# An adaLN block with a state-space mixer and eight experts: identity matmuls at the start, the first norm planned first, one more early slot, late loads in a new order

## The chip, the cores and the metric

The kernel runs on one core of one Trainium2 chip. The metric is the device time of one execution in microseconds. The core has five engines, each with its own instruction queue that it works off in order: PE (matmuls), DVE (vector), ACT (scalar and activation), POOL (GpSimd) and SP (which here only starts DMAs). In the trace PEld is PE's loading of the stationary operand.

## The reference

All data are float32. `x` holds B = 8 sequences of L = 512 tokens with D = 256 features; `c` holds one conditioning vector for each sequence.

```python
mod = (silu(c) @ wmod).reshape(8, 6, 1, 256)
sa, ca, ga, sb, cb, gb = (mod[:, i] for i in range(6))
ga, gb = (sign(g) * max(|g|, 0.25) for g in (ga, gb))     # with sign(0) = 1

h  = layernorm(x) * (1 + ca) + sa
x  = x + ga * attn(h)
h  = layernorm(x) * (1 + cb) + sb
x  = x + gb * ffn(h)

def attn(x):                                 # a state-space mixer, 512 inner features
    xn = layernorm(x) * gamma + beta
    u, z = split(xn @ W_in.T)                # 512 and 512
    xc = silu(depthwise_causal_conv(u, 4 taps) + conv_b)
    # state (16 numbers): s_t = s_{t-1} @ A.T + u_t @ Bm.T
    y  = (xc + s @ Cm) * sigmoid(z)
    return x + y @ W_out.T

def ffn(x):                                  # 4096 tokens, 8 experts, 1024 hidden features
    top_p, top_i = top_k(softmax(x @ wr + br), 2)
    gate = top_p[:, 0] / (top_p[:, 0] + top_p[:, 1])
    e = top_i[:, 0]                          # each token goes to one expert
    return gate * (gelu(x @ w1[e] + b1[e]) @ w2[e] + b2[e])
```

## The kernel before

**The plan.** Nearly the whole program is written against a `Plan` (line 30 on), an object that looks like the core and only records instructions with their tiles. `order()` (line 191) then makes a list schedule: it has a modelled length for each instruction, follows tile dependences, PSUM and SBUF buffers and a modelled DMA wire, and takes at each step, over all engines, the instruction that can start earliest, and among equal starts the one with the earliest due time. Due times are set in the code by `nc.due = ...` and handed back along dependences. Instructions are emitted sorted by their planned start; the chip does not see due times, only the order in each engine's queue. `plan.wanting(done=[...])` adds tiles that an instruction is to come behind in the plan. There are two plans: one for everything up to the router, one for the experts.

**First plan: mixer and router, batch by batch.** At the start `load_x`, the modulation weights `wm0`, `wm1` and the projection weights `wi`, `wo` are loaded. `three()` (line 482) makes the modulation vectors: for batch 0 on all 128 partitions at once (`s0`, tiles `pm`, `pg`, result `bc0`), and in `vectors()` (line 513) for all batches, into the scratch tensors `mod_d` and `modb_d`, from which later batches load their `bc`. `vectors()` makes the router's vectors too (`pf`, `modT`, `rw`, `rsum`, `wr2`). `states()` (line 590) prepares the state space: powers of A by repeated squaring (`at`, each step a PE product `pa` and a copy), tables `lt`, `lx`, `cs`, `wb`, `lm`, and `bw`, the product of `W_in` with `Bm`. It has 35 small copies on DVE. Then, for each batch, `stage_norm` (line 735) makes two layer norms (`xn`, `h`, then `xnT`, features on partitions; the power -1/2 runs on POOL), `stage_base` a base term, `stage_conv` projects `u` (tile `px`), convolves on DVE (`sv`) and scans the state, `stage_out` projects `z`, combines and multiplies with `W_out` (tile `po`), norms again (`xr`) and picks the expert (`oh`), and `stage_place` counts places and scatters the token numbers into `ids_d` with indirect DMAs from POOL, four for each batch, and stores the rows in `xp_d`. The code orders `states()`, `vectors()`, then the batches, with due times PERIOD = 36 us apart.

**Slots.** The expert part works in slots: a pair slot is 256 tokens of one expert, a single slot 128. For a slot, `name_tokens` (line 1023) loads its token numbers `ids` from `ids_d` on SP's queue, `rows_of` gathers the rows `xg` on POOL's, `expert_of` (line 1035) loads `w1t`, `b1t`, `b2t`, `w2t` (two megabytes) on SP's, `features` makes `hg` and transposes it to `hT` (tile `tp`), `layer1` multiplies into `ph` and takes gelu into `gl`, `layer2` multiplies into `py`, makes `ot` and scatters it to the output.

After FEW = 6 of 8 batches `early_table()` (line 958) already fixes the first NEARLY = 3 pair slots from the tokens seen so far. Slot 0's first layer is part of the first plan, and so are the gathers of slots 0 and 1. After batch 8 a late table is computed on DVE (tiles `cum`, `unit`, `done`, `mine`, `ef`, `ei`), and the other slots follow it: 13 pair slots and 4 singles always, three more singles under a condition. Weights have four buffers (`wts`), besides those of slot 0.

**Second plan.** `fetched(i)` (line 1150) is `expert_of` plus `rows_of`. `got` lists the slots fetched ahead; `work()` (line 1289) goes through the slots with `ahead = len(got)` slots in flight, names the tokens of one more, and writes for each slot `features` of the next, `layer1`, and `layer2` of the one before.

In the trace most instructions carry L154 or L159, the two lines of `Plan.add` that issue a recorded instruction (L154 where several calls are joined), so the tile names tell the groups apart. SP's dynamic loads carry their own lines: L1028 token numbers, L1041 `w1t`, L1048 `w2t`. A float32 matmul shows as two PE instructions.

Of the kernel before, what the change touches and what calls it, by code (L numbers as in the profile page):

```python
# [10 lines left out]
FP = mybir.dt.float32  # L11
# [7 lines left out]
P = 128  # L19
# [16 lines left out]
class Plan:  # L36
# [20 lines left out]
    def __init__(self, tc, last=None):  # L57

        self.tc, self.nc = tc, tc.nc
        self.free = {q: last.free[q] if last else 0.0 for q in self.REACH}  # L60
        self.ops, self.touched, self.tiles = [], {}, {}
        self.due, self.also, self.pairing = 0.0, ([], []), 0
        for name in self.QUEUES:
            setattr(self, name, self.Engine(self, name))

# [125 lines left out]
    def order(self):  # L191
        ops = self.ops
# [6 lines left out]
        start = [0.0] * len(ops)  # L199
# [11 lines left out]
        order, table = [], 2  # L211

        def may(o):

# [8 lines left out]
                at = max(at, sorted(slots[tag])[len(names) - 1])  # L223
            return at

        while len(order) < len(ops):
            best = None
            for q, l in ready.items():
                for o in l:
                    at = may(o)  # L230
                    if at is None:
                        continue
                    at = max(at, free[q])
                    if o.get("table") not in (None, table):
                        at += 1.3
                    if best is None or (at, o["due"]) < best[:2]:
                        best = (at, o["due"], o)
            assert best is not None, "no buffer for any instruction that could be next"
            at, _, o = best
# [8 lines left out]
            free[o["queue"]] = at + o["length"]  # L248
            end = at + o["length"]
            if o["size"]:  # L250
                if o["indirect"]:
                    end += 9.0
                else:
                    wire = max(wire, end) + o["size"] / 300e3
                    end = wire
            done[o["i"]] = end
            o["at"] = at
            order.append(o)
            for n in o["uses"]:
                if o["i"] in self.tiles[n][1]:  # L260
                    self.tiles[n][1].discard(o["i"])
                    left[n] -= 1
                    o_end = end + self.reach(o)
                    t = self.tiles[n][0]
                    self.ends = getattr(self, "ends", {})
                    self.ends[n] = max(self.ends.get(n, 0.0), o_end)
                    if left[n] == 0:
                        slots[t.tag].append(self.ends[n])
            for j in o["after"]:
                a = ops[j]  # L270
                start[j] = max(start[j], end + (0.05 if a["queue"] == o["queue"] and not o["size"] else self.reach(o)))
                missing[j] -= 1
                if missing[j] == 0:
                    ready[a["queue"]].append(a)
# [15 lines left out]
def adaln_mamba_moe_kernel(  # L290
# [28 lines left out]
    JB = BLK // P  # L319


    FEW, NEARLY = 6, 3
    assert (FEW * NT - E) // 2 + 1 >= NEARLY


# [105 lines left out]
    with tc.tile_pool(name="wa", bufs=1) as wa, tc.tile_pool(  # L431
# [158 lines left out]
        def states():  # L590


            for j in range(STEPS - 1):
                pa = ps_s.tile([DS, 2, DS], FP, name="pa", tag="ps")
                for s in range(2):
                    nc.tensor.matmul(
                        pa[:, s], lhsT=at[:, j, 1 - s], rhs=at[:, j, s], start=True, stop=True
                    )
                nc.vector.tensor_copy(at[:, j + 1], pa)
            i16 = ident[0:DS, 0:DS]  # L600
            a3t = wa.tile([DS, DS], FP, name="a3t")
            pa3 = ps_s.tile([DS, DS], FP, name="pa3", tag="ps")
            nc.tensor.matmul(pa3, lhsT=at[:, 0, 1], rhs=at[:, 1, 0], start=True, stop=True)
            nc.vector.tensor_copy(a3t, pa3)
            power = [i16, at[:, 0, 0], at[:, 1, 0], a3t, at[:, 2, 0]]


# [2 lines left out]
            nc.vector.memset(lt, 0.0)  # L610
            for i in range(CH):
                for j in range(i + 1):
                    nc.vector.tensor_copy(lt[:, i, j * SP : j * SP + DS], power[i - j])
                nc.vector.tensor_copy(lt[:, i, DS : 2 * DS], power[i + 1])
# [8 lines left out]
            for i, (l, r) in enumerate((  # L623
# [4 lines left out]
            nc.vector.tensor_copy(more[:, 0:5], pmo)  # L628
            pm28 = ps_s.tile([DS, DS], FP, name="pm28", tag="ps")
            nc.tensor.matmul(pm28, lhsT=at[:, 4, 0], rhs=more[:, 0], start=True, stop=True)  # L630
            nc.vector.tensor_copy(more[:, 5], pm28)
# [8 lines left out]
            nc.vector.tensor_copy(wb[:, :, DS:], pw1)  # L640

            gaps = [at[:, 5, 0], at[:, 6, 0], more[:, 3], at[:, 7, 0], at[:, 8, 0], more[:, 4]]
            lx = wa.tile([DS, len(gaps), 2 * DS], FP, name="lx")
            nc.vector.memset(lx, 0.0)
            for j, m in enumerate(gaps):
                nc.vector.tensor_copy(lx[:, j, DS:], m)
            ix = wa.tile([DS, 2 * DS], FP, name="ix")
            nc.vector.memset(ix, 0.0)
            nc.vector.tensor_copy(ix[:, DS:], i16)
            pm2 = ps_s.tile([2 * DS, len(gaps), 2 * DS], FP, name="pm2", tag="ps")  # L650
# [3 lines left out]
            nc.vector.tensor_copy(lm, pm2)  # L654

            wx = wxo[:, 1].rearrange("p (j d) -> p j d", j=KI)
            for g in range(KI // 2):
# [10 lines left out]
            pb = ps_s.tile([P, KD, DS], FP, name="pb", tag="ps")  # L668
# [6 lines left out]
            nc.vector.tensor_copy(bw[:, :, 0:DS], pb)  # L675

            return cs, wb, lm, bw

# [337 lines left out]
        def loads(fn, outs, ins, length):  # L1016

            if nc is plan:
                plan.call("sync", fn, outs, ins, length)
            else:  # L1020
                fn()

        def name_tokens(i):
            jb, at_ = tiles(i), where[i][1]

            def fn():
                o = chip.sync.value_load(at_, min_val=0, max_val=E * TOK)
                chip.sync.dma_start(  # L1028
                    out=ids[:, i, 0:jb],
                    in_=ids_d[bass.ds(o, jb * P), :].rearrange("(p j) o -> p (j o)", j=jb),  # L1030
                )
# [106 lines left out]
    with tc.tile_pool(name="g", bufs=2) as gp, tc.tile_pool(  # L1138
# [8 lines left out]
        nc.due = behind + 4 * SLOT  # L1147
        turn = count_from()

        def fetched(i, xg=None):  # L1150
            t = expert_of(
                i, wts.tile([P, KD, FF], FP, name="w1t"), wts.tile([P, KF, D], FP, name="w2t"),
                blk.tile([P, KF], FP, name="b1t"), blk.tile([P, D], FP, name="b2t"),
            )
# [12 lines left out]

        half = tab.tile([1, 2 * E], I32, name="half")
# [120 lines left out]
        def work(slots, got, begun=None):  # L1289
# [96 lines left out]
```

## Time and profile before

| | |
|---|---|
| median of 3 runs | 596.09 us (595.05 to 597.38) |
| the profiled execution | 595.11 us |
| its span in the profile | 593.2 us, so 1.9 us lie outside the span |
| PE busy | 564.6 us (95%), 2882 instructions |
| DVE, ACT, POOL busy | 351.0, 210.7, 209.4 us |
| mean granted clock of PE | 0.974 of full speed |
| DMA | 96.73 MB, 163 GB/s on average |

A line of the timeline reads: start, duration (both us), engine, line of the kernel, operation, output tile <- input tiles, shape, how many alike were merged, and in brackets how long the engine had idled before and what ended the idling. SPq is SP's DMA-issuing queue. In the page's slices one digit stands for 1/40 of the span (14.8 us), in tenths of busy time or, in the row of the clock, in tenths of full speed. Where PE is busy nearly always, the time is set by what PE has to do, by its idle stretches and by the clock that it is granted.

### The profile page before, as it was taken

The page shows a single profiled execution, that of the slowest core. Times are in us where ns is not written, and L with a number is a line of the kernel's source. Part 1 is how long each engine was busy: PE and PEld are TensorE (multiplying, and loading weights), DVE is VectorE, ACT ScalarE, POOL GpSimd, SP SyncE. Part 2 cuts the span into 40 slices and gives each one's busy share as a digit, 9 for nine tenths or more (in the row PEclk, how much of TensorE's full clock was granted, in tenths as well). Part 3 has the DMA queues.
Part 4 walks back from the last instruction along what each step waited for, and adds up shares of the span by engine and source line. Part 5 has one row for each costly group of instructions (what it writes and reads, how often), then busy time and mean ns, then how long its engine had stood idle before and what let it go on. Part 6 is the DMA issues. An engine that isn't in the chain of part 4 may idle for free. (4 is left out here: it accounts for less than half of the span.)

```text
span 593.2 us, 8692 instructions
## 1 busy us (share of the span) xinstructions
PE 564.6 (95%) x2882; PEld 430.7 (73%) x2882; DVE 351.0 (59%) x1087; ACT 210.7 (36%) x404; POOL 209.4 (35%) x334
## 2 busy tenths in 40 slices
PE   5999999999999999999999875999999999999996
PEld 2454766767575776767478764888988988988895
DVE  4879978988887678585876524434341533533212
ACT  2328544445463634341522220221322222232140
POOL 1422663636345461631334132432332222331111
PEclk9779999999999999999999896999999999999998
DMA  7347999310300101010645999699977887794000
GB/s 275 125 146 181 279 258 242 74 60 1 98 1 1 38 2 36 1 37 1 203 128 167 165 288 341 190 374 380 317 253 236 295 282 243 253 326 163 24 18 20
DMA packets 58703, 96.73 MB, mean 163 GB/s; under 512 B 9852, under 2 KB 41854, under 8 KB 58656
## 3 DMA queue, kind: packets, MB, share of 16 engines
q1 hardware_dynamic: 50720, 72.98, 41.2%
q0 software_dynamic: 7936, 23.17, 11.5%
q8 instruction: 24, 0.39, 0.4%
q14 instruction: 23, 0.19, 0.2%
HBM read 86.42 MB, written 22.81 MB: 184 GB/s over the span
## 5 line engine op out<-in xcount | busy, mean ns | idle before, releaser
L159 ACT ACTIVATE gl<-ph,b1t 128x256 f32<-128x256 f32 (+1 forms) x152 | 68.5, 452 | 187.9 <-PE ph L154 186.0
L154 PE MATMUL py<-w2t,gl 128*128 128x256 f32 x476 | 110.2, 384 | 0.0
L154 PEld LDWEIGHTS py<-w2t,gl 128*128 128x128 f32 x476 | 92.1, 193 | 13.1
L159 POOL DMA_INDIRECT out<-ot,ids x36 | 37.1, 1030 | 158.1 <-DVE ot L159 140.7
L159 DVE SCALAR_TENSOR_TENSOR sv<-u,pt,sv 128x512 f32<-128x512 f32 x96 | 77.1, 809 | 13.0 <-ACT sv L159 12.7
L159 PE MATMUL ph<-hT,w1t 128*128 128x256 f32 (+1 forms) x304 | 84.2, 359 | 0.0
L154 PE MATMUL ph<-hT,w1t 128*128 128x256 f32 (+1 forms) x304 | 84.2, 359 | 0.0
L159 DVE TENSOR_TENSOR ot<-py,b2t 128x256 f32<-128x256 f32 x34 | 14.4, 424 | 113.1 <-PE py L154 110.1
L159 PE MATMUL px<-xnT,wi 128*128 128x512 f32 x128 | 69.6, 626 | 0.0
L154 PE MATMUL px<-xnT,wi 128*128 128x512 f32 x128 | 66.0, 597 | 0.0
L159 POOL DMA_INDIRECT xg<-xp_d,ids x36 | 38.6, 1073 | 62.7 <-DMA ids<-ids_d 42.3
L154 PEld LDWEIGHTS ph<-hT,w1t 128*128 128x128 f32 x304 | 55.6, 191 | 6.3
L159 PEld LDWEIGHTS ph<-hT,w1t 128*128 128x128 f32 x304 | 55.1, 191 | 5.9
L159 POOL DMA_INDIRECT ids_d<-tok,row x32 | 34.7, 1084 | 36.1 <-DVE row L159 13.7
L154 PEld LDWEIGHTS px<-xnT,wi 128*128 128x128 f32 x128 | 24.6, 192 | 31.2 <-issue 31.2
L159 ACT COPY u<-px 128x512 f32<-128x512 f32 x32 | 18.7, 585 | 63.4 <-PE px L154 63.4
L159 ACT ACTIVATE tz<-px 128x512 f32<-128x512 f32 x32 | 19.1, 596 | 40.3 <-PE px L154 36.7
L159 PEld LDWEIGHTS px<-xnT,wi 128*128 128x128 f32 x128 | 21.3, 192 | 16.4 <-issue 14.6
L159 POOL TENSOR_TENSOR rs<-ve,nhalf 128x4 f32<-128x4 f32 x16 | 19.4, 1217 | 38.7 <-DVE ve L159 28.8
L159 DVE COPY hT<-tp 128x512 f32<-128x512 f32 (+1 forms) x20 | 12.7, 634 | 34.2 <-PE tp L154 33.9
L159 DVE TENSOR_TENSOR hg<-hg,xg 128x256 f32<-128x256 f32 x72 | 28.8, 422 | 1.2
L159 DVE TENSOR_TENSOR xr<-po,h 128x256 f32<-128x256 f32 x32 | 13.5, 421 | 25.6 <-PE po L154 25.3
(347 smaller groups left out, 947.4 us busy)
## 6 DMA issues: line engine op xcount, KB each, us to landing
w1t<-in_w SPq DMA_DIRECT2D x19, 1024.0 KB, 8.2
w2t<-in_w SPq DMA_DIRECT2D x19, 1024.0 KB, 5.6
xp_d<-modb_d SPq DMA_DIRECT2D x8, 1536.0 KB, 21.2
xp_d<-xr SPq DMA_DIRECT2D x8, 520.0 KB, 4.6
xt<-in_x SPq DMA_DIRECT2D x8, 512.0 KB, 11.6
bc<-mod_d SPq DMA_DIRECT2D x7, 384.0 KB, 3.5
b2t<-in_b SPq DMA_DIRECT2D x19, 128.0 KB, 8.3
w<-in_w SPq DMA_DIRECT2D x2, 1024.0 KB
```

The source lines that it names most:

```text
L154: me["calls"].append(lambda: getattr(getattr(self.nc, name), op)(*args, **kw))
L159: calls=[lambda: getattr(getattr(self.nc, name), op)(*args, **kw)],
```

## The change

1. `Plan.order()` gets two more settings. `hold = 24`: as long as an engine's earliest possible start lies before 24 us (planned time), it takes, among what can start within 0.3 us of that, the instruction with the earliest due time. `warm = (20.0, 7.8, 0.47, filler)`: before 20 us of planned time, each planned gap of PE is filled to 80% with matmuls of the identity with itself (256 columns, tile `pwarm`, read by nobody); a matmul is planned at 0.47 us, and before 7.8 us, where lengths are doubled, at 0.94.
2. `stage_norm(0)` is written first, with due time 20. `states()` follows, and `vectors()` and `stage_base(0)` come behind `xnT` of batch 0.
3. In `states()` the 35 copies move from DVE to ACT, and `pw1`, `pm2`, `pb` move from a PSUM pool of one buffer to that of `px` with three.
4. `NEARLY` goes from 3 to 4, so 12 pair slots are left to the late table.
5. Slot 1 is fetched first; then the numbers of the first late slot (now slot 4) are named, and slots 2 and 3 are fetched behind these in the plan. In `work()` each later slot's numbers are named behind the `w1t` of the slot fetched last.

```diff
@@ Plan.order()
-        while len(order) < len(ops):
+        while len(order) < len(ops) + fillers:
...
-                    if best is None or (at, o["due"]) < best[:2]:
-                        best = (at, o["due"], o)
+                    could.append((at, o["due"], o["i"], o))
+                if could:
+                    mine = min(could)
+                    if mine[0] < self.hold:
+                        mine = min((c for c in could if c[0] < mine[0] + 0.3), key=lambda c: c[1:3])
+                    if best is None or mine[:3] < best[:3]:
+                        best = mine
...
+            length = o["length"]
+            if self.warm and o["queue"] == "PE" and at < self.warm[0]:
+                slow = 2 if at < self.warm[1] else 1
+                n = int(0.8 * (at - free["PE"]) / (slow * self.warm[2]))
+                if n > 0:
+                    order.append(dict(i=-1, at=free["PE"], queue="PE", calls=[self.warm[3]] * n))
+                    fillers += 1
+                length *= slow
@@
-    FEW, NEARLY = 6, 3
+    FEW, NEARLY = 6, 4
@@ vectors()
             for half, to in ((0, mod_d), (1, modb_d)):
+                nc.due = (1 + 2 * half) * PERIOD
...
+            nc.due = 3 * PERIOD
@@ states(), 35 copies in all
-                nc.vector.tensor_copy(at[:, j + 1], pa)
+                nc.scalar.copy(at[:, j + 1], pa)
...
-            pw1 = ps_s.tile([P, SPAN[0], DS], FP, name="pw1", tag="ps")
+            pw1 = ps_x.tile([P, SPAN[0], DS], FP, name="pw1", tag="px")
@@
-        def name_tokens(i):
+        def name_tokens(i, behind=()):
...
-            loads(fn, [ids[:, i, 0:jb]], [at_, *id_views[: FEW * NT]], 0.8)
+            loads(fn, [ids[:, i, 0:jb]], [at_, *id_views[: FEW * NT], *behind], 0.8)
@@
         PERIOD = 36.0
+        pwarm = ps_o.tile([P, 2, P], FP, name="pwarm", tag="po")
+        twice = ident.unsqueeze(1).to_broadcast([P, 2, P])
+        plan.hold = 24.0
+        plan.warm = (20.0, 7.8, 0.47, lambda: chip.tensor.matmul(
+            pwarm, lhsT=ident, rhs=twice, start=True, stop=True
+        ))
+        nc.due = 20.0
+        t = stage_norm(0)
+        nc.due = 1e6
         cs, wb, lm, bw = states()
-        rw, rsum, wr2 = vectors()
+        with nc.wanting(done=[t["xnT"]]):
+            rw, rsum, wr2 = vectors()
+            nc.due = 3 * PERIOD
+            stage_base(t)
         for b in range(B):
             nc.due = (b + 3) * PERIOD
-            t = stage_norm(b)
-            stage_base(t)
+            if b:
+                t = stage_norm(b)
+                stage_base(t)
@@
-        got = [slot0, fetched(1, pre[1])] + [fetched(i) for i in range(2, NEARLY)]
+        got = [slot0, fetched(1, pre[1])]
@@ work()
-                    name_tokens(slots[n + ahead + 1])
+                    name_tokens(slots[n + ahead + 1], [got[-1][1]] if nc is plan else ())
@@
         name_tokens(slots[NEARLY])
+        got += [fetched(i, None, [ids[:, NEARLY, :]]) for i in range(2, NEARLY)]
```

More of the change, by code (lines that the diff above doesn't have):

```diff
@@ L62, in __init__ @@
         self.due, self.also, self.pairing = 0.0, ([], []), 0
+        self.hold, self.warm = 0.0, None
         for name in self.QUEUES:
@@ L210, in order @@
         done = [0.0] * len(ops)
-        order, table = [], 2
+        order, table, fillers = [], 2, 0
         def may(o):
@@ L224, in may @@
             return at
-        while len(order) < len(ops):
+        while len(order) < len(ops) + fillers:
             best = None
             for q, l in ready.items():
+                could = []
                 for o in l:
@@ L235, in order @@
                         at += 1.3
[L236 to L237 removed]
+                    could.append((at, o["due"], o["i"], o))
[5 more added lines that the diff above has]
+                        best = mine
             assert best is not None, "no buffer for any instruction that could be next"
[L239 removed]
+            at, _, _, o = best
             table = o.get("table") or table
@@ L247, in order @@
             ready[o["queue"]].remove(o)
-            free[o["queue"]] = at + o["length"]
-            end = at + o["length"]
+            length = o["length"]
[6 more added lines that the diff above has]
+                length *= slow
+            free[o["queue"]] = at + length
+            end = at + length
             if o["size"]:
@@ L603, in states @@
             nc.tensor.matmul(pa3, lhsT=at[:, 0, 1], rhs=at[:, 1, 0], start=True, stop=True)
-            nc.vector.tensor_copy(a3t, pa3)
+            nc.scalar.copy(a3t, pa3)
             power = [i16, at[:, 0, 0], at[:, 1, 0], a3t, at[:, 2, 0]]
@@ L612, in states @@
                 for j in range(i + 1):
-                    nc.vector.tensor_copy(lt[:, i, j * SP : j * SP + DS], power[i - j])
-                nc.vector.tensor_copy(lt[:, i, DS : 2 * DS], power[i + 1])
+                    nc.scalar.copy(lt[:, i, j * SP : j * SP + DS], power[i - j])
+                nc.scalar.copy(lt[:, i, DS : 2 * DS], power[i + 1])
             cs = wa.tile([P, CH, DI], FP, name="cs")
@@ L627, in states @@
                 nc.tensor.matmul(pmo[:, i], lhsT=l, rhs=r, start=True, stop=True)
-            nc.vector.tensor_copy(more[:, 0:5], pmo)
+            nc.scalar.copy(more[:, 0:5], pmo)
             pm28 = ps_s.tile([DS, DS], FP, name="pm28", tag="ps")
             nc.tensor.matmul(pm28, lhsT=at[:, 4, 0], rhs=more[:, 0], start=True, stop=True)
-            nc.vector.tensor_copy(more[:, 5], pm28)
+            nc.scalar.copy(more[:, 5], pm28)
             back = [i16, at[:, 2, 1], at[:, 3, 1], more[:, 0], at[:, 4, 1], more[:, 1], more[:, 2],
                     more[:, 5]]
-            pw1 = ps_s.tile([P, SPAN[0], DS], FP, name="pw1", tag="ps")
+            pw1 = ps_x.tile([P, SPAN[0], DS], FP, name="pw1", tag="px")
             for g in range(SPAN[0]):
@@ L639, in states @@
             nc.vector.memset(wb, 0.0)
-            nc.vector.tensor_copy(wb[:, :, DS:], pw1)
+            nc.scalar.copy(wb[:, :, DS:], pw1)
             gaps = [at[:, 5, 0], at[:, 6, 0], more[:, 3], at[:, 7, 0], at[:, 8, 0], more[:, 4]]
@@ L645, in states @@
             for j, m in enumerate(gaps):
-                nc.vector.tensor_copy(lx[:, j, DS:], m)
+                nc.scalar.copy(lx[:, j, DS:], m)
             ix = wa.tile([DS, 2 * DS], FP, name="ix")
             nc.vector.memset(ix, 0.0)
-            nc.vector.tensor_copy(ix[:, DS:], i16)
-            pm2 = ps_s.tile([2 * DS, len(gaps), 2 * DS], FP, name="pm2", tag="ps")
+            nc.scalar.copy(ix[:, DS:], i16)
+            pm2 = ps_x.tile([2 * DS, len(gaps), 2 * DS], FP, name="pm2", tag="px")
             for j in range(len(gaps)):
@@ L653, in states @@
             lm = wa.tile([2 * DS, len(gaps), 2 * DS], FP, name="lm")
-            nc.vector.tensor_copy(lm, pm2)
+            nc.scalar.copy(lm, pm2)
             wx = wxo[:, 1].rearrange("p (j d) -> p j d", j=KI)
@@ L667, in states @@
             nc.vector.memset(bw, 0.0)
-            pb = ps_s.tile([P, KD, DS], FP, name="pb", tag="ps")
+            pb = ps_x.tile([P, KD, DS], FP, name="pb", tag="px")
             for k in range(KD):
@@ L674, in states @@
                     )
-            nc.vector.tensor_copy(bw[:, :, 0:DS], pb)
+            nc.scalar.copy(bw[:, :, 0:DS], pb)
             return cs, wb, lm, bw
@@ L1148, in adaln_mamba_moe_kernel, with fetched @@
         turn = count_from()
-        def fetched(i, xg=None):
+        def fetched(i, xg=None, behind=()):
             t = expert_of(
                 i, wts.tile([P, KD, FF], FP, name="w1t"), wts.tile([P, KF, D], FP, name="w2t"),
-                blk.tile([P, KF], FP, name="b1t"), blk.tile([P, D], FP, name="b2t"),
+                blk.tile([P, KF], FP, name="b1t"), blk.tile([P, D], FP, name="b2t"), behind,
             )
```

## The prediction

> **What bounds the kernel now.** I read the page first. Section 1 and the slices of section 2 say that PE sets the time, and where it does not.
>
> ```profile
> PE 564.6 (95%) x2882; PEld 430.7 (73%) x2882; DVE 351.0 (59%) x1087; ACT 210.7 (36%) x404; POOL 209.4 (35%) x334
> ...
> PE   5999999999999999999999875999999999999996
> ...
> PEclk9779999999999999999999896999999999999998
> ```
>
> PE is busy all the time but for three places: the first slice, slices 22 to 24 and the last. The granted clock drops in the same region twice. So I cut the span at these places in the table of windows (stretch, its length, then PE, PEld, DVE, ACT, POOL busy, granted clock, DMA share, GB/s).
>
> ```profile
> 0.00:60.00 60.00, 51.29 (x243) 26.24 (x244) 45.06 (x159) 25.67 (x44) 17.86 (x52) 0.89 0.59 183
> 60.00:320.00 260.00, 257.46 (x1384) 179.45 (x1385) 204.54 (x653) 115.56 (x207) 118.23 (x211) 1.00 0.32 87
> 320.00:382.00 62.00, 50.23 (x221) 42.30 (x220) 28.27 (x104) 12.32 (x27) 20.50 (x21) 0.89 0.89 238
> 382.00:548.00 166.00, 166.00 (x838) 147.68 (x837) 62.65 (x151) 47.73 (x106) 45.50 (x44) 1.00 0.85 286
> 548.00:593.20 45.20, 39.64 (x203) 35.00 (x201) 10.45 (x23) 9.42 (x22) 7.34 (x8) 0.97 0.06 20
> ```
>
> From 60 to 320 and from 382 to 548 PE idles 2.5 us in 426: nothing is to be had there except fewer matmuls, and the change leaves their number alone. What the change can win lies in 0 to 60 (8.7 us idle) and in 320 to 382 (11.8 us idle), plus the slow clock in both. The tail it does not touch. Then I read the timeline of each.
>
> The start:
>
> ```profile
> 9.89 2.08 PE L159 MATMUL pm<-wm,s 128*128 128x512 f32 x2
> ...
> 10.00 0.18 DVE L159 COPY at<-pa 16x32 f32<-16x32 f32 x1 [2.33 <-PE pa L154]
> 10.11 0.14 DVE L159 SCALAR_TENSOR_TENSOR nm<-mv,rs 128x4 f32<-128x4 f32 x1
> ...
> 11.76 1.79 PE L154 MATMUL pm<-wm,s 128*128 128x512 f32 x2
> ...
> 31.14 0.78 ACT L159 ACTIVATE xnT<-tp_a,pt 128x512 f32<-128x512 f32 x1 [1.71 <-PE tp_a L154]
> ...
> 37.47 2.05 PE L159 MATMUL px<-xnT,wi 128*128 128x512 f32 x2
> ```
>
> The first batch's normalised features `xnT` are whole at 31.9, the first projection `px` runs at 37.5. Two `pm` pairs start 1.87 us apart; two `px` pairs of the same 128x512 shape at 47.59 and 48.44 start 0.85 apart. So PE ran at half rate around 10 us although the clock column of those slices shows no drop. The recorded drops are 0.58 from 19.9 to 28 and 0.62 from 33 to 42. Loss by half rate: 5.6 busy us from 7.8 to 13.5 give 2.8; 8.1 x 0.42 = 3.4; 9.0 x 0.38 = 3.4; together 9.6. With the idle 8.7, PE gives away 18.3 us in the first 60.
>
> The change-over to the experts:
>
> ```profile
> 325.97 0.98 POOL L159 DMA_INDIRECT ids_d<-tok,row  x1 [0.30 <-issue]
> ...
> 337.88 1.22 PE L159 MATMUL py<-w2t,gl 128*128 128x256 f32 x2 [2.45 <-DMA w2t<-in_w]
> ...
> 343.26 1.43 SPq L1028 DMA_DIRECT2D ids<-ids_d  x2
> ...
> 345.48 0.38 SPq L1041 DMA_DIRECT2D w1t<-in_w  x1
> ...
> 348.79 1.05 POOL L159 DMA_INDIRECT xg<-xp_d,ids  x1 [14.26 <-DMA ids<-ids_d]
> ...
> 360.45 0.47 PE L159 MATMUL tp<-ident,hg 128*128 128x128 f32 x1 [7.62 <-DVE hg L159]
> ```
>
> The last scatter of token numbers is issued at 326.0 and lands at 343.0, 17.0 later; only then can SP load the numbers of the first late slot (slot 3), POOL gather its rows, and DVE make `hg`. PE has finished slot 2's first layer by 353 and waits to 360.4. Slot 1 had waited 2.5 for `w2t`, whose load stood in the same DMA queue as slot 2's weights. Afterwards PE is slow: clock 0.79 in 335 to 343 (5.55 busy x 0.21 = 1.2) and 0.62 in 360 to 371 (8.85 x 0.38 = 3.4). Given away here: 11.8 + 4.6 = 16.4 us.
>
> **The start, costed.** Four edits act together: the norm of batch 0 is planned first (due 20, choice by due time until 24), identity matmuls fill PE's planned gaps until 20, 35 small copies go from DVE to ACT, and `vectors()` and `stage_base(0)` wait for `xnT`. I walk the chain to `xnT` with its own durations: `xt` at 5.36, statistics to 7.29, power on POOL 1.04 to 8.5, `nm` at 8.7 (it ran at 10.11 because DVE stood before the copy `at<-pa`), `xn` 2.07 to 10.9. `bc` needs `pm` and `pg` of `s0`: `wm` is there at 7.9, four and four passes at the full rate 1.7 + 0.9, so `bc` no longer comes last (it came at 13.6). Two products 2.5 to 13.4, statistics 2.3, power 1.2, `nm` 0.2, `xn` 2.1, transposes and `xnT` 1.7: 20.9, with an issue gap 21.2, against 31.9.
>
> PE cannot be filled with useful work till then. What does not need `xnT`: `pm`, `pg` 2.6, transposes of `wi` 1.8, `pq` 3.4, `pb` 3.4, `pw1` 1.9, `pm2` 0.6, the `pa` chain and `pmo` 3.1, together 16.8. So at least 21.2 - 16.8 = 4.4 us stay lost, and some 11 if only 10 us of it are ready (`cmt` lands at 14, the `pa` chain is eight round trips); I take the middle, 7.7. Half rate may come back once the fillers stop: none of it or 6.8 (the two recorded drops); I take 3, since dense `px` now follow at once. Gain 18.3 - 7.7 - 3 = 7.6, bounds 0.5 and 13.9.
>
> Side costs, inside these bounds. A filler has 256 columns; the nearest row, `ph` of 128x256, takes 0.43 at full rate and 0.85 slow, and that is the most one can hold up a ready instruction. The copies free DVE of 7.3 us (2.3 of it two stalled `lx`); on ACT no such copy is shown: bounds 0.1 to 0.59 (the 128x512 copy), I take the 0.22 of the nearest size (`ct`), 35 x 0.22 = 7.7 us beside 25.7 busy of 60. Behind a waiting copy on ACT stands `xn`, as `nm` stood on DVE. Behind the new wait of `vectors()` stands `mod_d`, stored at 33.2 before; from 21.2 on, PE 2.6 and five DVE steps of 0.4 give about 27, so batch 1's `bc` is not late. `pw1`, `pm2`, `pb` in the three-buffer PSUM pool and `pwarm` in the output pool: nothing, since `po` needs the second buffer only after 60; half a us each if a `px` had to wait.
>
> The Trainium skill, "TensorE: Matmul & The Clock Gate", Part 1, says that about 3.4 us of sustained matmuls release the clock and an idle window takes it back; it also puts the ramp at under 1% of a usual span, an estimate of 5.9 us here, where the rows give 9.6. By the page the start could win 3.7 us less at its ceiling, and the sum below would end near 580.
>
> **The change-over, costed.** `NEARLY` 4 gives PE one more slot (16 `ph` and 16 `py` pairs of 0.43, 13.8 us) whose tokens are known from the early table. That covers 353 to 360.4 fully: the first late slot is now needed two slots after slot 2. Slot 2's weights no longer compete with slot 1's `w2t`, so that wait goes too. But slots 2 and 3 now load behind the numbers of slot 4 in SP's queue, which waits for the scatter. Without slot 2's load in the way I let the last scatter land 10.8 to 13.2 us after 326.0, as in two quiet batches (163.7 and 234.9): 337 to 339. Then ids, then `w1t`(2), 5.0 to land as at 345.48: 342.7 to 345. PE wants it at 346.4 - 2.5 - 1.2 = 342.7. `w2t`(2) follows by 2 us and took 13.8 in this stage: 353 to 355, wanted at 342.7 + 6.9 = 349.6. So 1 to 6 us of new waiting. Two more gathers on POOL (1.04 + 0.31 each) may stand before the last power and push the table by 2.7; a loaded landing may add more: bounds 1 and 10, I take 4. Gain 16.4 - 4 = 12.4, bounds 6.4 and 15.4. The other ids loads now alternate with weights. Before, 13 of them held SP from 354.0 to 377.1 and no PE wait came of it, so this alone is worth nothing; it keeps slot 5's weights (issued 377.9, used near 403) ahead of a PE that comes 16 us earlier.
>
> Sum: 595.11 of the profiled execution (span 593.2 and 1.9 around it) - 7.6 - 12.4 = 575.1; the median of the runs is 1.0 higher, so 576.
>
> **Rivals.**
> - *The slower one: slot 2's weights become the bound.* Place: SP's queue from 326 to 367. If POOL's gathers push the scatter by 2.7 and it still takes 17.0, ids go out at 346; `w1t`(2) at 346.7, with the 20.2 us that slot 2's took here before, lands at 367: 24 us of waiting plus 2 of slow clock against 16.4 now. It decides from a landing at 366 if the start gains 7.6; with a start of 3 it gives 596.1 + 9.6 - 3 = 603. Against: the 20.2 was two slots' weights at once. Chance 0.10.
> - *A half-lost change-over*: the weights come 10 to 12 us late. 596.1 - 7.6 - 5 = 583. For: slot 3's `w2t` took 13.8 in this stage. Chance 0.13.
> - *The start gives nothing*: ACT stands in front of PE round trips and `xn` comes late, or fillers delay the `pa` chain. For: `nm` lost 1.5 us in just this way on DVE. 596.1 - 12.4 = 584. Chance 0.12.
> - *Both eat each other up*: within the 0.5% (3 us) that a measurement here can tell from no change. Chance 0.03.
> - The forecast, 576, with 568 to 585 of its own: 0.62. That the extra slot could be missing is excluded: six batches give 24 tiles, at least nine full pairs over eight experts.
>
> **How the numbers follow.** Faster 0.62 + 0.13 + 0.12 = 0.87, the same 0.03, slower 0.10. The range 566 to 590 takes in the forecast and both halves and leaves out the last two cases and a little below.
>
> **What would show it.** Right: a first `xnT` at 20 to 23 and `px` soon after; `pm` pairs 0.85 apart; scatters of each batch 5 to 10 us earlier; no PE wait for `hg` near 353; SP's order w(1), ids, w(2), w(3); a wait of PE for `w1t` or `w2t` of slot 2 of a few us. Wrong: `xn` late behind ACT copies, a clock of 0.6 still in 20 to 40, or a PE gap over 10 us at slot 2.

## The result, and the profile after

The changed kernel takes 620.59 us (median of 4 runs, 618.01 to 623.7) against 596.74 (4 runs, 595.05 to 597.93): the ratio is 1.0404, 95% interval 1.0348 to 1.046. It is slower by 4%, where 3% faster was forecast. Ratios here compare undisturbed runs with undisturbed runs of the kernel before on the same chip, so they can differ a little from the quotient of two medians. The profiled execution took 623.7 us, its span is 621.9.

The page of after, PE's row and its two rows of slices (15.5 us each):

```profile
PE 576.5 (93%) x2894; PEld 438.3 (70%) x2894; DVE 358.5 (58%) x1052; ACT 214.6 (35%) x439; POOL 214.1 (34%) x330
...
PE   8989999960699999999999999899999999999996
...
PEclk9775999995799999999999999899999999999998
```

Slice 1 went from 5 to 8, as it should. The dip at 22 to 24 of before is gone. But there is a new hole in slices 9 to 11 (124 to 171 us; PE stands idle from 134 to 160), where before was solid, and a stretch of slow clock in slices 2 to 4. The table of windows (the columns are those of the prediction) gives the sizes:

```profile
0.00:60.00 60.00, 54.33 (x239) 31.93 (x240) 41.41 (x121) 26.39 (x72) 19.83 (x55) 0.76 0.38 130
60.00:320.00 260.00, 230.91 (x1215) 156.68 (x1214) 188.29 (x561) 103.57 (x186) 106.24 (x174) 0.94 0.36 76
320.00:382.00 62.00, 60.30 (x299) 46.54 (x297) 45.40 (x170) 20.06 (x37) 25.83 (x43) 1.00 0.66 180
```

In 0 to 60 PE is busy 3 us more, but at a mean clock of 0.76 instead of 0.89. In 60 to 320, where I had put no change at all, 29 us are idle instead of 2.5. Two stages were read wrongly: the start itself, and a stage that the change does not seem to touch. The timeline of the start did what its steps said:

```profile
7.51 1.10 PE L160 MATMUL pm<-wm,s 128*128 128x512 f32 x2 [0.32 <-DMA wm<-in_wmod]
...
8.45 1.02 PE L155 MATMUL pm<-wm,s 128*128 128x512 f32 x2
...
19.17 1.52 ACT L160 ACTIVATE xnT<-tp_a,pt 128x512 f32<-128x512 f32 x2
...
25.04 1.12 PE L160 MATMUL px<-xnT,wi 128*128 128x512 f32 x2
```

The `pm` pairs start 0.94 us apart instead of 1.87, `xnT` is whole at 20.7 instead of 31.9, the first `px` runs at 25.0 instead of 37.5. Yet the first scatter of batch 0 is issued at 100.5 instead of 96.3, that of batch 1 at 168.6 instead of 130.9. The hole lies between the two. SP's queue of after, with the second half of the modulation vectors, `modb_d`, and what follows it:

```profile
78.59 0.29 SPq L160 DMA_DIRECT2D modb_d<-mod  x1
80.21 29.42 SPq L160 DMA_DIRECT2D xp_d<-modb_d  x7
109.68 18.63 SPq L160 DMA_DIRECT2D bc<-mod_d  x1
128.41 4.57 SPq L160 DMA_DIRECT2D xp_d<-xr  x1
133.09 7.12 SPq L160 DMA_DIRECT2D xt<-in_x  x1
```

and the same two steps in the queue of before:

```profile
36.31 0.29 SPq L159 DMA_DIRECT2D modb_d<-mod  x1
...
41.91 29.03 SPq L159 DMA_DIRECT2D xp_d<-modb_d  x7
```

Once `modb_d` is stored, seven copies of it (1.5 MB each, one row for every token of a sequence) go out together, because the plan takes what can start first. In before that happened at 42, in the shadow of batch 0. In after half 1 becomes ready only with `xnT`, beside batch 0's own work, and the plan put its matmuls behind that: on PE the last of them ends at 76.0 (30.5 in before). Their due time of 108 us is no later than before; there the broadcasts, due with batch 0 at 108, handed theirs back to them. So the store came 42 us later, and a token load `xt` stood behind the seven. DVE's line in the timeline shows what that does:

```profile
154.69 0.43 DVE L160 BATCH_NORM_STATS2 st<-xt 128x6 f32<-128x256 f32 x1 [25.85 <-DMA xt<-in_x]
```

This is a statistic for a later batch, worked ahead. It stands in DVE's queue in front of batch 1's convolution (`sv`) and state (`v`), so batch 1 waits with it: among PE's waits `pd <- v` (PE's products with the state) takes 26.3 us in one piece.

The change-over did about what was said. POOL's last scatter, then SP and POOL:

```profile
362.53 0.98 POOL L160 DMA_INDIRECT ids_d<-tok,row  x1 [0.30 <-issue]
...
374.29 0.70 PE L160 MATMUL py<-w2t,gl 128*128 128x256 f32 x2 [0.85 <-DMA w2t<-in_w]
375.92 0.34 SPq L1048 DMA_DIRECT2D ids<-ids_d  x1
377.06 0.37 SPq L1061 DMA_DIRECT2D w1t<-in_w  x1
378.56 1.29 POOL L160 DMA_INDIRECT xg<-xp_d,ids  x1 [7.58 <-DMA ids<-ids_d]
379.85 0.37 SPq L1061 DMA_DIRECT2D w1t<-in_w  x1
```

The scatter has landed 13.4 us after its issue (17.0 before), the numbers go ahead of slot 2's and 3's weights, and PE waits 0.9 us for `w2t` and 1.9 for `w1t` instead of 7.6 for `hg`. The last scatter is 36.6 us later than in before, the end of the span 28.7: behind the last scatter some 8 us are won back. That this is the late part's doing is not shown by it (see a3 below).

### The profile page after: what moved, and what is told of

Same layout as the page of the kernel before. It is cut to its first block, busy times and chain, and to the rows that moved or that the text cites. A ratio compares the mean times of both kernels' runs of the same rounds, so it can differ in the third digit from the quotient of the medians.

```text
span 621.9 us, 8717 instructions
## 1 busy us (share of the span) xinstructions
PE 576.5 (93%) x2894; PEld 438.3 (70%) x2894; DVE 358.5 (58%) x1052; ACT 214.6 (35%) x439; POOL 214.1 (34%) x330
## 4 chain that ended last, share of the span: by engine, by line
PE 62%; DMA 22%; DVE 9%; issue 3%; SPq 2%; POOL 1%; ACT 1%; POOLq 0%; ACTq 0%; DVEq 0%
DMA xg<-xp_d,ids 9%; PE py L155 9%; PE po L155 8%; PE px L160 8%; PE px L155 7%; PE ph L160 5%; PE ph L155 5%; DMA xt<-in_x 5%; PE pc L155 3%; DVE sv L160 3%; PE po L160 3%; DMA ids<-ids_d 3%; PE pd L155 2%; DMA w1t<-in_w 2%; DMA ids_d<-tok,row 2%
## 5 line engine op out<-in xcount | busy, mean ns | idle before, releaser
L160 DVE SCALAR_TENSOR_TENSOR sv<-u,pt,sv 128x512 f32<-128x512 f32 x96 | 71.3, 760 | 1.2 <-ACT sv L160 1.0
L160 PE MATMUL px<-xnT,wi 128*128 128x512 f32 x128 | 71.5, 641 | 0.5 <-DVE mod L160 0.3
L155 PE MATMUL px<-xnT,wi 128*128 128x512 f32 x128 | 66.9, 604 | 0.0
L160 POOL DMA_INDIRECT ids_d<-tok,row x32 | 41.7, 1302 | 41.2 <-DVE row L160 29.7
L160 PEld LDWEIGHTS px<-xnT,wi 128*128 128x128 f32 x128 | 21.8, 195 | 18.2 <-issue 16.3
L160 POOL TENSOR_TENSOR rs<-ve,nhalf 128x4 f32<-128x4 f32 x16 | 17.4, 1089 | 43.3 <-DVE ve L160 31.5
L160 PE MATMUL pd<-v,lm 32*32 32x120 f32 (+1 forms) x32 | 6.5, 286 | 26.8 <-DVE v L160 26.8
```

Source lines behind the costliest of these rows:

```text
L155: me["calls"].append(lambda: getattr(getattr(self.nc, name), op)(*args, **kw))
L160: calls=[lambda: getattr(getattr(self.nc, name), op)(*args, **kw)],
```

## The experiments

Theory A: half 1 of the modulation, made late, puts the seven broadcasts in front of a token load. Theory B: the start itself is to blame (fillers, copies on ACT, half clock). Theory C: the late part. Line numbers of experiments differ from the kernel's by the lines that they add.

**First set: one thing undone, one part alone.** `a1_modb_due` gives both halves the same due time; `a2_late_alone` is the kernel before with parts 4 and 5 of the change only; `a3_early_alone` is the changed kernel with `NEARLY = 3` and the old order of the late loads; `a4_modb_late` is the kernel before with half 1 alone moved behind batch 0's convolution.

```diff
# a1
-                nc.due = (1 + 2 * half) * PERIOD
+                nc.due = PERIOD
# a4, in the loop over the batches, behind stage_conv(t)
+            if b == 0:
+                with nc.wanting(done=[t['sv']]):
+                    mods(1, modb_d)          # half 1, taken out of vectors()
```

> The changed kernel with one line altered: both halves of the modulation vectors are due at 36 us, so modb_d is stored soon after mod_d and not at 78.6. Theory A (the late modb_d moves the ten megabytes of row broadcasts from 42 to 80 us, where a token load stands behind them and DVE and then PE wait 26 us): the wait for xt near 130 to 155 us goes, 620.6 - 30 = about 590. Theory B (the start itself is to blame: fillers, copies on ACT, 24 us at half clock, and the broadcast only stands by): 612 to 622. Theory C (the late part costs the time): 615 to 622.

> The kernel before with the late edits alone: NEARLY 4, slots 2 and 3 loaded behind the first late numbers, names behind weights. Theory A: the last scatter came 36.6 us later in the changed kernel and the end only 28.7, so the late part gains about 8: 589 (my forecast had 12.4, 584). Theory B: the same. Theory C: slower than 597.

> The changed kernel with NEARLY 3 and the old order of the late loads: the early edits alone. Theory A and theory B: 620.6 + 8 = about 628, with the wait for xt at 130 to 155 us as before. Theory C: 597 or less.

> The kernel before, with nothing else changed than that the second half of the modulation vectors is made behind batch 0's convolution, so modb_d is stored later. Theory A: if the store comes past about 60 us, a token load stands behind the broadcasts and the time grows, up to 30 us: 605 to 627; if it comes by 50, nothing happens, 597. Theory B: 597 wherever the store comes.

| | median, us | ratio to before | interval |
|---|---|---|---|
| a1_modb_due | 595.02 | 1.0063 | 1.0029 to 1.0097 |
| a2_late_alone | 585.24 | 0.9874 | 0.9814 to 0.9935 |
| a3_early_alone | 616.89 | 1.0426 | 1.0363 to 1.0489 |
| a4_modb_late | 607.64 | 1.02 | 1.0117 to 1.0283 |

C falls: the late part alone (a2) makes the fastest version of all, 585.24, faster than both kernels. A holds for most of the loss: one due time takes 1.0404 to 1.0063, and the kernel before gets slower once its half 1 is made late. But a1 is still slower than a2 by 1.0063/0.9874 = 1.019, some 11 us, where the early part was to gain 7.6. That part was open. a3 missed its 628: with the old late part it is as slow as the changed kernel (1.0426 against 1.0404). Its wait for `xt` is shorter (20.6 us against 25.9), and from its last scatter, issued at 354.24, to the end of its span it takes 260.1 us, like after (259.4) and not like before (267.2). So the 8 us that after wins back behind the last scatter also come without the late part, and what the late part is worth rests on a2 alone.

**Second set: what at the start?** From a1: `b1_h` lets the vectors wait for `h` only; `b2_no_fill` leaves the fillers out; `b3_gap_fill` adds nine identity matmuls behind `pv`. `b4_fill_alone` is a2 with the fillers as the only early edit.

```diff
# b1
-        with nc.wanting(done=[t["xnT"]]):
+        with nc.wanting(done=[t["h"]]):
# b2
-        plan.warm = (20.0, 7.8, 0.47, lambda: ...)
# b3, in stage_conv, behind pv
+            if b == 0:
+                plan.call("tensor", lambda: [chip.tensor.matmul(pwarm, lhsT=ident, rhs=twice, ...)
+                                             for _ in range(9)], [], [pv], 9 * 0.45)
```

> The changed kernel with both halves of the modulation stored early (as in a1_modb_due), and the vectors wait only for the first modulated features h instead of xnT, so that the small matmuls of the router (pf, pw of wo, half 1 of pm and pg) run before the first px and not after the gap that follows it. Theory 'small matmuls': PE stays at half clock from 44 to 66 because they stand there with few columns; dense px and pq now follow the gap at once, the clock is back some 4 us later, about 8 to 10 us less than a1: 585 to 588, ratio 0.98 to 0.99, first scatter near 95. Theory 'gap': PE is still idle before batch 0's pd for want of v on DVE, so the half clock comes all the same: 593 to 598, ratio 1.00 to 1.01. Theory 'fillers or copies': unchanged, 593 to 598.

> a1_modb_due without the seven identity matmuls; the rest of the early part stays. If the fillers do what they are for (a full clock from 8 us on), pm runs at half rate again and some 3 us are lost: 597 to 600, ratio 1.01. If they only stand in the way of ready work: 588 to 592, ratio 0.99 to 1.00. If they are worth nothing either way, which I hold likeliest, since PE then lacks work till xnT anyhow: 593 to 597, ratio 1.005.

> a1_modb_due with nine identity matmuls of 256 columns put on PE behind batch 0's pv, so that PE is busy through the gap of 3.8 us in which it waits for v. Theory 'gap': that gap takes the clock to half for the 22 us after it, which costs 11 us; with the gap filled the granted clock stays at 1.0 from 41 on and the time is 584 to 588, ratio 0.98 to 0.99, first scatter near 93. Theory 'small matmuls' or 'the clock falls for another reason': the half clock comes at 44 to 48 nonetheless, 594 to 599, ratio 1.00 to 1.01.

> The kernel before with the late part (as in a2_late_alone, 585.24) and of the early part the identity matmuls alone: no first norm ahead, no wait of the vectors, copies on DVE. If the fillers by themselves save the half rate of 7.8 to 13.5 (2.8 us, the one size that the traces give): 580 to 583, ratio 0.975 to 0.98. If work that follows is not ready sooner, or the clock falls at 20 all the same: 584 to 587, ratio 0.985 to 0.99. If they delay the pa chain: 588 and more.

| | median, us | ratio to before | interval |
|---|---|---|---|
| b1_h | 597.77 | 1.0092 | 1.0054 to 1.0131 |
| b2_no_fill | 599.78 | 1.0142 | 1.0102 to 1.0182 |
| b3_gap_fill | 594.02 | 1.0045 | 1.0022 to 1.0069 |
| b4_fill_alone | 615.85 | 1.038 | 1.0325 to 1.0435 |

None of them gave back the 11 us. b1 speaks against the router's narrow `pf`: they ran early, at 22 to 24, and the half clock came all the same from 46 to 63, beginning in a gap of 3.1 us on PE; the time is in the range that the text gave for 'gap' and for 'fillers or copies'. b3 was inconclusive, since the plan put its nine matmuls at 25.5 and not into the gap. b2 says that the fillers are worth 0.8% where they are; but part of that may again be the queue, for DVE in b2 waits 9.1 us for an `xt` at 95.7 and in a1 0.7 at most. b4 is the surprise: 615.85 where 580 to 587 was expected, by edits that only add matmuls nobody reads. Its timeline, SP's queue and DVE:

```profile
69.61 0.29 SPq L160 DMA_DIRECT2D modb_d<-mod  x1
...
137.82 1.08 DVE L160 BATCH_NORM_STATS2 st<-xt 128x6 f32<-128x256 f32 x3 [24.23 <-DMA xt<-in_x]
```

The doubled lengths in the plan moved the last `pm` of half 1 from 28 (a2) to 67 us, and theory A struck in a kernel where nobody had touched the vectors. So A has six points, and in a4 nothing but half 1 was moved:

| | half 1 stored at, us | longest wait of `st` for `xt`, us |
|---|---|---|
| a1 | 34.7 | 0.7 |
| before | 36.3 | none |
| a4 | 58.5 | 16.3 |
| b4 | 69.6 | 24.2 |
| a3 | 74.9 | 20.6 |
| after | 78.6 | 25.9 |

**Third set: the clock, and the queue.** A ledger of the first 110 us of a1 and a2 from the windows (two-us steps: idle, and busy x (1 - clock)): a2 has 10.7 idle and 5.1 by slow clock, a1 7.3 and 15.9, and 5.2 us of a1's busy time are fillers. PE's timeline of a1 shows the long one:

```profile
44.97 0.60 PE L160 MATMUL pd<-v,wb 128*32 128x127 f32 x2 [3.81 <-DVE v L160]
...
48.82 4.84 PE L155 MATMUL pf<-sT,wm 128*128 128x8 f32 x22
...
61.12 2.08 PE L160 MATMUL px<-xnT,wi 128*128 128x512 f32 x2
...
66.40 1.12 PE L155 MATMUL px<-xnT,wi 128*128 128x512 f32 x2
```

After a gap of 3.8 us PE never idles again, but 24 `pf` instructions of eight columns take 5.3 us, and the `px` pairs at 61 still run at half rate; only at 66 they take 1.1 us. In before wide `px` pairs stood between the narrow work; with `xnT` early they are all used up ahead of the gap. `c1_gap` keeps PE's order and puts nine fillers exactly into the gap; `c2_gap_pf` adds six between the `pf`; `d2_copies_dve` is a1 with the 35 copies back on DVE and `pw1`, `pm2`, `pb` back in their old PSUM pool; `e1_no_behind` is the changed kernel, broadcasting the first half's vectors (stored near 30) in place of the late ones, so that the transfers are the same and the numbers in the rows are not the reference's.

```diff
# c1, in Plan.emit(); c2 also has one filler in front of every second call of pf
             for o in order:
+                if (o.get("out") or "").startswith("pd_0_0"):
+                    for _ in range(9):
+                        self.warm[3]()
# e1
-                    out=xp_d[n * L : (n + 1) * L, OWN:ROW], in_=modb_d[n].partition_broadcast(L)
+                    out=xp_d[n * L : (n + 1) * L, OWN:ROW], in_=mod_d[n].partition_broadcast(L)
```

> a1_modb_due with PE's order kept as it is and nine identity matmuls of 256 columns (9 x 0.43 = 3.9 us) put just in front of batch 0's first pd, where a1 waits 3.8 us for v (b3_gap_fill's nine had been placed at 25.5, not there). Theory 'gap': the idle time takes the clock; filled, it stays full to 66 and about 11 us are saved: 584 to 587, ratio 0.98 to 0.99. Theory 'small matmuls': the clock falls all the same once pd and pf (16 and 24 narrow instructions) run, some 5 us later than in a1; 2 to 3 us saved: 592 to 594, ratio 1.000 to 1.004. Theory 'copies on ACT or another cause': 595 and more.

> c1_gap, and besides one identity matmul of 256 columns in front of every second of the twelve narrow pf matmuls (6 x 0.43 = 2.6 us of added work), so that PE never has narrow work alone for over 2 us between 41 and 54. Theory 'small matmuls': the clock stays at full from 41 on, 11 us saved and 2.6 paid: 586 to 589, ratio 0.985 to 0.993. Theory 'gap': as c1 plus 2.6: 587 to 590 with c1 at 584 to 587. Theory 'another cause': the clock falls all the same and the 2.6 are paid: 597 to 600, ratio 1.01.

> a1_modb_due with the 35 small copies, and the three PSUM tiles, back where the kernel before had them (DVE). If the copies on ACT are to blame (xn behind them, sv's silu late, so v late for pd): 588 to 591, ratio 0.99 to 1.00. If they help as they were meant to: 598 to 602, ratio 1.01 to 1.02. If the clock decides, the time goes by the length of the half-rate stretch in 40 to 70: per us of it half a us against a1's 22.5 us.

> The changed kernel as it is, half 1 of the modulation computed and stored as late as it was there (near 78), but the eight broadcasts read the first half's vectors instead, which are there at about 30: the numbers in the rows are not the reference's, the transfers are the same in number and size. So only what stands behind the late store on SP is taken away. Theory A (the token load behind the broadcasts is the loss): no wait for xt near 130 to 155 and 593 to 598, ratio 1.000 to 1.010. Rival (the late matmuls and copies of half 1 themselves cost it, or the traffic does): 612 to 621, ratio 1.035 to 1.05.

| | median, us | ratio to before | interval |
|---|---|---|---|
| c1_gap | 596.3 | 1.0063 | 1.0034 to 1.0093 |
| c2_gap_pf | 600.97 | 1.0136 | 1.0082 to 1.019 |
| d2_copies_dve | 595.22 | 1.0053 | 1.003 to 1.0076 |
| e1_no_behind | 600.44 | 1.013 | 1.0095 to 1.0165 |

e1: with only the queue relieved, 1.0404 falls to 1.013, half 1 being computed just as late (stored at 77.7). It is not free of the wait: its broadcasts go out from 39 on, and DVE waits 8.9 and 5.8 us for `xt` at 47 and 91. The copies do not matter (d2 against a1). c2 was to take 586 to 589 and took 600.97, its runs from 596 to 609; that is a little above the 597 to 600 forecast for 'another cause', although half rate cost 8.5 us in its first 110 and not a1's 15.9. c1's time is also where the text had put 'another cause' (595 and more), but its timeline says why:

```profile
42.95 4.15 PE L1124 MATMUL pwarm<-ident 128*128 128x256 f32 x18
...
49.08 2.60 PE L155 MATMUL pf<-sT,wm 128*128 128x8 f32 x22
...
56.85 2.08 PE L160 MATMUL px<-xnT,wi 128*128 128x512 f32 x2
...
94.29 0.43 DVE L160 BATCH_NORM_STATS2 st<-xt 128x6 f32<-128x256 f32 x1 [6.72 <-DMA xt<-in_x]
...
100.15 0.64 PE L160 MATMUL pk<-oh,lower 128*128 128x32 f32 x2 [3.69 <-DVE xr L160]
```

`pf` takes 2.6 us instead of 4.8, half rate lasts 7 us (54 to 61) instead of 24 (43 to 67), and batch 1's first `px` runs at 83.89 instead of 88.82: 4.9 us won. Then DVE waits 6.7 us for `xt`, which stands behind the same seven broadcasts even when these go out at 40, PE waits behind DVE, and the first scatter is at 104.8 against a1's 103.3. The gain was there and was given back at the next limit. (c2 waits 4.1 us at the same place, b3 4.0.)

**Fourth set: both limits off.** The broadcast of a batch's vectors is planned behind the rows `xr` of the batch before, in the changed kernel (f1), in c1 (f2), in a2 (f3) and in a1 (f4):

```diff
+                with nc.wanting(done=[xr]):
                     nc.sync.dma_start(
                         out=xp_d[n * L : (n + 1) * L, OWN:ROW], in_=modb_d[n].partition_broadcast(L)
                     )
```

> The changed kernel with one edit: the broadcast of a batch's modulation into the rows waits, in the planner, for the rows xr of the batch before, so that the eight broadcasts stand one behind each batch's rows on SP and no longer seven together in front of xt; half 1 is computed as late as before (near 75). Theory A (seven broadcasts in front of a token load): no wait for xt over 3 us anywhere and 588 to 596, ratio 0.99 to 1.005. Rival (half 1's late matmuls, or the late store itself, cost the time): 610 and more, ratio over 1.03.

> c1_gap (clock full to 54, PE 4.9 us ahead of a1 at batch 1's first px) with the broadcasts put one behind each batch's rows. In c1 that lead was lost again in a wait of DVE of 6.7 us for xt at 94. Theory 'two limits': the half clock and the load behind the seven broadcasts each cap the start, so that taking both away gives 585 to 589, ratio 0.98 to 0.99, with batch 0's first scatter at 95 to 99. Theory 'something else on DVE': the scatter stays at 103 to 105 and the time at 593 to 597, ratio 1.00 to 1.01.

> a2_late_alone (the late loads in their new order alone) with the broadcasts put one behind each batch's rows. Its xt loads were late for nobody by more than 1 us, so theory A gives no change: 583 to 586, ratio 0.983 to 0.992. If the seven broadcasts cost by the memory traffic they make in 42 to 110: 579 to 582, ratio 0.975 to 0.98.

> a1_modb_due with the broadcasts put one behind each batch's rows; nothing done about the clock. With f2 it says what each limit is worth. Theory 'two limits': PE stays 4.9 us behind f2, xt no longer late: 590 to 594, ratio 0.99 to 1.003. If the load alone capped the start: 585 to 589, the same as f2; if it is the clock alone: 594 to 597, the same as a1.

| | median, us | ratio to before | interval | first scatter, us |
|---|---|---|---|---|
| f1_after_spread | 592.76 | 1.0025 | 0.9993 to 1.0056 | 95.7 |
| f2_gap_spread | 591.02 | 0.9984 | 0.996 to 1.0008 | 97.8 |
| f3_late_spread | 589.08 | 0.9945 | 0.9919 to 0.9972 | 96.5 |
| f4_due_spread | 594.65 | 1.0036 | 0.9998 to 1.0073 | 102.6 |

SP's queue of f1, with half 1 as late as in the changed kernel:

```profile
73.83 0.29 SPq L160 DMA_DIRECT2D modb_d<-mod  x1
90.99 0.37 SPq L160 DMA_DIRECT2D xp_d<-xr  x1
91.42 0.60 SPq L160 DMA_DIRECT2D xp_d<-modb_d  x1
92.13 0.87 SPq L160 DMA_DIRECT2D xt<-in_x  x1
```

f1 settles A: one edit to the order of the broadcasts takes the changed kernel from 1.0404 to 1.0025, and DVE's longest wait for an `xt` behind the first load is 2.1 us. Late vectors as such cost nothing: f4, with early ones, is no faster (1.0036). f2 brought its scatter to 97.8, inside the 95 to 99 of "two limits", but not its time: 591 instead of 585 to 589, since PE then waits 3.8 us at 319.8 for slot 0's weights, whose load stands behind the last broadcast at 288.8. f4 came out above its range for 'two limits' (590 to 594) and in that for 'the clock alone' (594 to 597), close to both. f3, the control, was to stay at a2's time and lost too (0.9945 against a2's 0.9874), with a wait of PE of 5.9 us at slot 0. PE's lines in f2 and in f3:

```profile
319.75 1.22 PE L160 MATMUL ph<-hT,w 128*128 128x256 f32 x2 [3.78 <-DMA w<-in_w]
```

```profile
320.19 1.22 PE L159 MATMUL ph<-hT,w 128*128 128x256 f32 x2 [5.88 <-issue]
```

Putting the broadcasts late seems to move their cost to the end of the batches; in f3 the profile names no releaser for the wait, so there this is an inference. Against this control the early part comes out at f4/f3 = 1.009 as it is and f2/f3 = 1.004 with its gap filled. It gains nothing. Whether it costs 11 us (a1 against a2) or these 5 is not settled, since f3 pays 5.9 us at slot 0 where f4 pays 2.5.

The late part's own size: a2 gains 1 - 0.9874, or 7.5 us (interval 3.8 to 11). Its row of the windows for the change-over, and PE's three waits there:

```profile
320.00:382.00 62.00, 56.16 (x254) 47.64 (x253) 26.56 (x97) 12.68 (x28) 16.79 (x17) 0.97 0.95 312
```

```profile
343.97 0.70 PE L159 MATMUL ph<-hT,w1t 128*128 128x256 f32 x2 [1.48 <-DMA w1t<-in_w]
352.36 0.30 PE L159 MATMUL tp<-ident,hg 128*128 128x128 f32 x1 [1.22 <-DVE hg L159]
354.65 0.33 PE L159 MATMUL tp<-ident,hg 128*128 128x128 f32 x1 [1.88 <-DVE hg L159]
```

5.8 us idle and 1.7 by slow clock (56.16 x 0.03) remain of the 16.4 that before gave away here. The other 8.9 fit the measured 7.5 and its interval.

## Why the prediction was wrong, step by step

- **The failed step is the new wait of `vectors()`.** The text followed one store: "Behind the new wait of `vectors()` stands `mod_d`, stored at 33.2 before", and ended with "batch 1's `bc` is not late". That was right as far as it went. `vectors()` issues a second store, `modb_d`, and the text did not follow it: the wait put its matmuls behind batch 0's, and on it hang seven planned DMAs of 1.5 MB on the queue that also carries the tokens. Against the 20 us that the sum gained stands a wait of 26.3 us that is no term of it. The page before had the row (`xp_d<-modb_d` x8, 1536 KB) and the timeline had SP held for 29.0 us at 41.9; I had read both as harmless where they lay and never asked where they would lie. a4, e1 and f1 show this step alone: from 1.0404 to 1.0025 by f1, 22.5 us of 595.
- **The start's half rate was mis-sized.** Of 18.3 us given away, "7.7 idle" and "3 half rate" were to stay. With half 1 early (a1) 7.3 idle stayed, 5.2 of fillers came on top, and half rate took 15.9 in 0 to 110, far over the 6.8 that was taken as its ceiling. The reason given, "dense `px` now follow at once", was wrong in its second part: dense `px` follow `xnT` at once and are used up before the gap, so narrow work comes last. c1 shows that the clock is worth 4.9 us there, and that another limit, the load behind the broadcasts, stands right behind it. Even with both off (f2) the start gains nothing, where 7.6 us were forecast.
- **The change-over was right in mechanism, and too large.** SP's order, the covered gap and the short waits came as told; 7.5 us instead of 12.4, inside the bounds of 6.4 to 15.4. The term "I take 4" of new waiting measures 7.5 in a2 (5.8 idle, 1.7 slow clock; that the gain is 7.5 too is chance): the wait for `hg` did not vanish (3.1 us). Slot 4's rows, gathered from 341.4 on beside weight loads at some 400 GB/s, reach DVE at 350.9; that the loads delay them was not tested. The 13.8 us given for a `w2t` "in this stage" belong to one issued at 392.7, behind it; the two that the trace times in the stage took 17.6 and 18.5. PE waited 0.9 us for `w2t` in after all the same.
- **What was right:** the walk to `xnT` (21.2 told, 20.7 measured), `pm` at full rate, the copies' harmlessness (d2), the order of the loads. Each was a local time; the end was set by a queue that the walk did not pass.
- **The rivals** held three ways for a term to be smaller and one for slot 2's weights. None asked what the moved step itself issues. The 0.87 for faster came from varying the sizes of the terms on the list, not from looking for a term that was missing.

## What to carry to other kernels

When a step is moved in a planned schedule, list every instruction that depends on it, DMAs first, and ask what stands behind them in their queue at the new time: the value of a transfer's place is often the shadow that it lies in. A change that only adds work to the plan can move such a transfer too (b4), so after any edit compare the order of the DMA queue first. And when one limit is taken away and nothing moves, look for the second in the timeline of the same run (c1), then take both away (f2).

## What the runs showed of the hardware

- PE's clock can stay at half for 24 us. In a1 the windows give 0.50 from 43 to 67; PE's idle stretch of 3.8 us ends at 45.0 and it is busy from there on. Till 61 what runs is mostly narrow (8 to 32 columns or rows, and `pq` with 16 rows, beside eight 128x128 transposes). The clock is back after 5 us of 128x512 pairs, in c1 after four. The Trainium skill, "TensorE: Matmul & The Clock Gate", Part 1, says about 3.4 us of sustained matmuls open the gate and an idle window shuts it. Here 16 us of mostly narrow matmuls without a gap (45 to 61) did not open it, and in c1 it shut at 54 with no idle time ahead, behind `pd` and `pf`. That narrow work is the cause is an inference from where the drops lie, and `pf` alone is not it (b1). c2, made to test it, had the same order up to 48 as c1 and was at half rate from 43 to 47, inside the fillers, where c1 was at full; through its `pf` with fillers between them it was at full rate. Where exactly the clock falls is not fixed by the order alone, and this stays open.
- The seven broadcasts of 1.5 MB hold SP for 29 us and, in after, a load of 0.5 MB behind them is there for DVE 74 us after the first was issued (80.2 to 154.7). The Trainium skill, "DMA: Bandwidth & Descriptors", section "Queues, rings and completion order", says that on each DMA engine a queue's descriptors are taken in ring order; the load's place behind them fits that.
